# Scan products on quadrants of TensorE, and three steps shifted, in a two-layer perceiver kernel

## The chip, the cores and the metric

The kernel runs on one core of one Trainium2 chip. The metric is the device time of one execution in microseconds (us), taken as the median of several runs. A core has a matrix engine (TensorE, PE in the profile, with PEld for its weight loads), a vector engine (VectorE, DVE), an activation engine (ScalarE, ACT), a general engine (GpSimd, POOL) and a queue engine (SyncE, SP) that here issues most of the transfers. Each engine works through its own instructions in order; semaphores join them. Matrix products go to PSUM, a small memory in banks of 512 f32 per partition, and are read from there by DVE or ACT.

## The reference

Sixteen batches of 64 latent tokens (128 wide, `x`) pass through two layers. Each layer is a cross attention to a context of 1601 tokens, a sequence model (a scan) and a feed-forward part; each part adds to `x`. The first layer has a scan of 16 states per channel and a mixture of experts with a small attention of its own, the second a scan with 4 heads and a feed-forward part with 4-bit quantization. Cut to what matters here:

```python
x = x + L0_xattn(ctx, layernorm(x), ...)     # 16 heads, latents attend to context and latents
x = x + L0_attn(layernorm(x), ...)           # scan of the first layer
x = x + L0_ffn(layernorm(x), ...)            # 4-head attention over 64 tokens, then 8 experts, 2 used
x = x + L1_xattn(ctx, layernorm(x), mask, ...)
x = x + L1_attn(layernorm(x), ...)           # scan of the second layer, below
x = x + L1_ffn(layernorm(x), ...)            # 4-bit quantized gate, up, down

def step(h, inp):                            # L1_attn, one token, per batch and head
    x_t, dt_t, B_t, C_t = inp
    h = exp(A * dt_t) * h + dt_t * B_t * x_t
    y_t = einsum('bhpn,bhn->bhp', h, C_t) + D * x_t
    return h, y_t
```

The scan of the second layer can be written without a loop. For tokens s <= t of the same batch, y_t is the sum over s of (C_t . B_s) times exp(A times the sum of dt over s+1..t) times dt_s x_s. The kernel does it in this form: a matrix of decays, a matrix of products C times B, their product where s <= t in the same batch, and one matrix product with dt x.

## The kernel before

Two batches of 64 tokens make one chunk of 128 tokens; there are eight chunks. All matrix products are in f32, and each shows up as two records of PE and two of PEld.

**The attention is the beat.** `run` counts steps n. One group is a batch and half of its heads; it has 13 steps, one per tile of 128 context rows, and there are 64 groups, 32 per layer. In a step `scores` makes one 128 by 512 product (tile `s`, three PSUM buffers of their own), DVE keeps a running maximum `R` and ACT copies the scores to `st`. A maximum is turned and spread (`tm`, `mb`), `weigh` subtracts and exponentiates, and 21 steps (`LAG`) after the scores `average` weighs the values: four products of 128 by 129 (tile `av`). The big `st` tiles have twelve buffers under the tag `st2`.

**The rest is put between.** Everything else is written as generators. `prep` holds those with a step at which they begin (weights folded, context loaded and normalized, queries). `between` holds the first layer's `scan0` and `moe`, for four groups of two chunks each, and then the second layer's `scan1` and `ffn`, for chunks 0-1, 2-3, 4-5, 6 and 7. Those in `between` run strictly one after the other. A step adds a budget, at most 2.0 of it is kept; a generator that yields a number takes that much of it, and one that yields a tuple (`HOP1` is `(1,)`, `HOP3` is `(3,)`) is not called again before so many steps have passed. `prep`'s generators are called once per step, and a tuple makes them skip steps. The `behind` context places what a generator issues behind the matmuls of the attention already issued, so its place in each engine's order follows from the step in which it is called. Loads go to SP and have no such tie to the attention. After the last step the remaining generators are run out as a tail: the last chunk's `scan1` and `ffn` run alone there, with filler matmuls (`fill`) between.

**PSUM for all but attention's scores and averages** is `tp`: one tag, three buffers of one bank each. Scans, experts, transposes and folds share it. A fourth request waits until an earlier tile is read.

**Lines that the change touches.** Lines 274 to 287 (`setup_rest`) build two 128 by 128 masks on POOL: `upto` (1 where s <= t in the same batch) and `after` (1 where s > t in the same batch). Lines 323 to 352 (`fold`) load a pair of raw weights with `raw_pair` and multiply them per head; `fold_vo(0)` begins at step 9, makes W_v times W_o for the first layer in four turns, and waits `HOP3` between a turn's loads and its products. Each pair sits in one of the twelve `st2` buffers. The first reader of the folded product is the first attention output, at step 81. In `moe`, lines 974 to 986 make queries (`mq`), keys (`mk`) and values (`mv`) of its small attention one after the other, each in a `tp` tile that ACT copies out. `scan1` does this for a chunk c:

- line 1272: `af` = `after` times A dt, a head per 128 columns (DVE)
- lines 1295 to 1301: `gr` = B times C with heads of the same half i of the partitions in one `tp` tile; DVE multiplies by `upto` into `gm`
- lines 1304 to 1310: `seg` = `af` times `upto`, the sums of A dt; ACT exponentiates into `af`
- line 1320: `gm` = `gm` times `af` (DVE)
- lines 1326 and 1329: `sy` = `gm` times `xd` (dt x), added to `y`

In the last chunk the exponential and line 1320 are done in two halves (`parts`), two heads each. Since a chunk holds two batches, half of each 128 by 128 block of `af` and `gm` is zero.

## Time and profile before

| | us |
|---|---|
| median of 3 runs | 1975.37 (1974.5 to 1977.61) |
| the profiled execution | 1973.36 |
| its span, first to last instruction | 1971.6 |
| steps 0 to 416, layer 1's scores begun | 11.5 to 952.2 |
| last score | 1902.9 |
| `moe`, first group | 475.2 to 577.7 |
| `moe`, last group | 1352.5 to 1452.4 |
| `scan1`, chunks 0-1, 2-3, 4-5 begin | 1459.8, 1567.9, 1741.2 |
| last `scan1` | about 1936 to 1954.5 |

The profile is of one execution. Its page gives the busy time of each engine and the costliest groups of instructions by line; the trace behind it can be asked for the busy time in a stretch, for the instructions in order of time (start, length, engine, line, operation, output and inputs, shape, and in brackets how long the engine stood idle before and for whom), and for the chain of work that ended last. A matmul line merges the records of one source line; `x8` is four f32 matmuls. Matmuls are pipelined, so the length of a merged line reaches beyond the start of what follows; what a block of matmuls costs PE is read from start to start.

### The profile page before, as it was taken

The numbers are of one execution on the slowest core, as the hardware profiler recorded it, in microseconds if no ns is written. First come the engines' busy times: TensorE is split into PE (matmuls) and PEld (weight loads), VectorE is DVE, ScalarE is ACT, GpSimd is POOL, SyncE is SP. The second block draws the span as 40 slices with busy tenths as digits, with TensorE's granted clock in tenths as the row PEclk, the third lists the DMA queues.
The fourth block names the chain that finished last, engine by engine and source line by source line (L and its number), as shares of the span: only waits on it lengthen the run. The fifth ranks groups of instructions, "written<-read, shape, count | busy, mean of one in ns | idle before, by whom it ended". The sixth has DMA issues, their size and how long they took to land. (4 is left out here: it accounts for less than half of the span.)

```text
span 1971.6 us, 32642 instructions
## 1 busy us (share of the span) xinstructions
PE 1931.2 (98%) x11987; PEld 1478.8 (75%) x11987; DVE 1582.9 (80%) x3029; ACT 1383.5 (70%) x2638; POOL 512.3 (26%) x579
## 2 busy tenths in 40 slices
PE   8999999999999999999999999999999999999998
PEld 5777777677777767777777777777778777787786
DVE  6977776987878887876998878898786978778875
ACT  5888787887868878666776657776665665766651
POOL 5211122543123452121452202542110111101000
PEclk9999999999999999999999999999999999999999
DMA  6121112322122221221221112221120210201000
GB/s 184 46 68 51 39 54 77 85 67 70 35 76 85 66 77 53 67 78 59 77 82 54 41 40 64 70 58 54 49 67 1 58 37 19 59 18 37 23 1 23
DMA packets 146223, 111.86 MB, mean 57 GB/s; under 512 B 13827, under 2 KB 132367, under 8 KB 146063
## 3 DMA queue, kind: packets, MB, share of 16 engines
q1 hardware_dynamic: 145518, 109.51, 19.1%
q8 instruction: 95, 1.56, 0.3%
q14 instruction: 66, 0.53, 0.1%
q10 hardware_dynamic: 544, 0.26, 0.0%
HBM read 81.28 MB, written 27.41 MB: 55 GB/s over the span
## 5 line engine op out<-in xcount | busy, mean ns | idle before, releaser
L760 PEld LDWEIGHTS av<-kv,st 128*128 128x128 f32 x6656 | 870.0, 192 | 376.6 <-issue 357.5
L760 PE MATMUL av<-kv,st 128*128 128x129 f32 x6656 | 881.8, 275 | 4.0 <-DVE aq L769 4.0
L697 PE MATMUL s<-qT,kvT 128*128 128x512 f32 x1664 | 859.3, 599 | 7.4 <-ACT st L712 5.5
L748 ACT ACTIVATE st<-st 128x1024 f32<-128x1024 f32 (+1 forms) x448 | 444.3, 996 | 120.7 <-DVE st L747 114.1
L747 DVE TENSOR_TENSOR st<-st,mb 128x1024 f32<-128x1024 f32 (+1 forms) x448 | 503.7, 1134 | 17.9 <-PE mb L739 17.9
L710 ACT ACTIVATE st<-s,mcol 128x512 f32<-128x512 f32 x416 | 283.2, 684 | 191.3 <-DVE R L705 167.6
L712 ACT COPY st<-s 128x512 f32<-128x512 f32 x416 | 240.0, 580 | 133.6 <-DVE R L707 121.4
L705 DVE SCALAR_TENSOR_TENSOR R<-s,mcol,R 128x512 f32<-128x512 f32 x352 | 262.2, 745 | 43.9 <-PE s L697 42.4
L707 DVE TENSOR_TENSOR R<-s,R 128x512 f32<-128x512 f32 x352 | 241.0, 685 | 61.9 <-PE s L697 59.8
L697 PEld LDWEIGHTS s<-qT,kvT 128*128 128x128 f32 x1664 | 254.5, 192 | 21.6 <-ACT st L712 10.3
L613 POOL TENSOR_TENSOR kv<-kv,vec 128x384 f32<-128x384 f32 (+1 forms) x128 | 131.8, 1050 | 149.5 <-PE kt L672 36.2
L809 POOL TENSOR_TENSOR aq<-aq,rd 128x512 f32<-128x512 f32 x63 | 74.4, 1181 | 341.4 <-DVE rd L808 329.9
L913 POOL TENSOR_TENSOR db<-sc_u,bb 128x512 f32<-128x512 f32 x64 | 83.7, 1310 | 120.2 <-DVE h L924 63.4
L930 POOL TENSOR_TENSOR sc_y<-sc_y,h 128x512 f32<-128x512 f32 x60 | 81.9, 1365 | 116.6 <-DVE h L929 100.0
L924 DVE TENSOR_TENSOR_SCAN h<-da,db 128x512 f32<-128x512 f32 x64 | 91.8, 1434 | 0.5 <-ACT da L912 0.5
L663 ACT ACTIVATE kv<-kv,coff,crstd 128x128 f32<-128x128 f32 x182 | 76.2, 490 | 6.0 <-POOL coff L660 6.0
L769 DVE SCALAR_TENSOR_TENSOR aq<-xeb,ee,av 128x129 f32<-128x129 f32 x252 | 76.3, 341 | 0.0
L654 ACT ACTIVATE scr<-kv,cmean 128x128 f32<-128x128 f32 x182 | 72.7, 399 | 2.8 <-DVE cmean L650 0.6
L135 POOL TENSOR_TENSOR crstd<-cvar,neghalf 128x13 f32<-128x13 f32 x14 | 34.2, 2440 | 138.1 <-DVE cvar L658 137.7
L490 PE MATMUL q<-xnT,wqk 128*128 128x128 f32 x512 | 68.1, 276 | 0.8 <-ACT qT L499 0.8
L490 PEld LDWEIGHTS q<-xnT,wqk 128*128 128x128 f32 x512 | 62.7, 192 | 4.1 <-issue 1.6
L681 ACT ACTIVATE kvT<-kvT,vcol 128x768 f32<-128x768 f32 (+1 forms) x62 | 58.2, 959 | 3.9 <-DMA xhT<-kvT 3.9
(419 smaller groups left out, 1896.7 us busy)
## 6 DMA issues: line engine op xcount, KB each, us to landing
bb<-bcd SPq DMA_DIRECT2D x64, 256.0 KB, 4.4
xh<-kv SPq DMA_DIRECT2D x16, 832.0 KB, 4.7
kv<-xh SPq DMA_DIRECT2D x16, 832.0 KB, 5.6
kvT<-xhT SPq DMA_DIRECT2D x16, 800.0 KB, 4.6
xhT<-kvT SPq DMA_DIRECT2D x15, 800.0 KB, 3.4
kv<-in_ctx_dram SPq DMA_DIRECT2D x15, 768.0 KB, 5.6
ew<-in_e1T_dram SPq DMA_DIRECT2D x36, 64.0 KB, 1.9
ew<-in_e3T_dram SPq DMA_DIRECT2D x36, 64.0 KB, 2.0
```

What stands on the lines that cost most here:

```text
L490: nc.tensor.matmul(t[:, k * P:(k + 1) * P], self.wqk[:, g * 4 + k, :], xnT, start=True, stop=True)
L613: nc.gpsimd.tensor_tensor(kv[:, lo:hi, :D], kv[:, lo:hi, :D], self.row(self.vec[:, w1, :], [P, hi - lo, D]), ALU.mult)
L697: mm = nc.tensor.matmul(s, self.kv_of[lay, b][1][:, i * P:(i + 1) * P], q, start=True, stop=True)
L705: mx = nc.vector.scalar_tensor_tensor(R, s, mc, last, ALU.add, ALU.max)
L707: mx = nc.vector.tensor_tensor(R, s, last, ALU.max)
L710: ev = nc.scalar.activation(st, s, AF.Identity, bias=mc)
L712: ev = nc.scalar.copy(st, s)
L747: nc.vector.tensor_tensor(st, st, self.row(mb, [P, n, NQ]), ALU.subtract)
L748: nc.scalar.activation(st, st, AF.Exp)
L760: nc.tensor.matmul(grp["av", j][:, k, :], st, self.kv_of[lay, b][0][:, i, :], start=(i == 0 and k == 0), stop=(i == NT - 1 and k == 1))
L913: nc.gpsimd.tensor_tensor(db, u, self.row(bb[:, 0, s % 2, :], both), ALU.mult)
L924: nc.vector.tensor_tensor_scan(flat(h), flat(da), flat(db), 0.0, ALU.mult, ALU.add)
```

## The change

In `scan1` the zero half of the blocks is no longer made. Masks, `af` and `gm` keep 64 columns per head: row p holds token p of its chunk, and the columns are the 64 tokens of p's own batch. The products `gr`, `seg` and `sy` are issued per batch b: the operands of batch b lie on partitions 64 b to 64 b + 63, and the output goes to the same partitions. So each of them becomes twice as many products with 64 columns of weights (`gr`: i chooses the input partitions and b the output partitions; `seg` and `sy`: b chooses both). `gr` takes both of its `tp` tiles before its first product. The last chunk's halves (`parts`) are gone. The numbers yielded are smaller (0.7 to 0.4 per chunk for `af`, 0.9 to 0.6 for `gr`, 0.8 to 0.5 for line 1320), and a `HOP1` stands between the first and the second chunk's `gr`.

In `moe` a yield of 0.3 and a `HOP1` stand between keys and values. In `fold` the first layer's W_v waits five steps instead of three between loads and products. `setup_rest` makes the two masks in 128 by 64 form, with two selects of 64 by 64 each.

```diff
-        self.upto = self.cst([P, P], "upto")
-        nc.gpsimd.memset(self.upto, 1.0)
-        nc.gpsimd.affine_select(
-            out=self.upto, in_=self.upto, compare_op=ALU.is_ge, fill=0.0, base=0,
-            pattern=[[1, P]], channel_multiplier=-1,
-        )
-        nc.gpsimd.memset(self.upto[0:64, 64:128], 0.0)
...
+        self.upto, self.after = self.cst([P, L], "upto"), self.cst([P, L], "after")
+        for t, op, sign in ((self.upto, ALU.is_ge, 1), (self.after, ALU.is_gt, -1)):
+            nc.gpsimd.memset(t, 1.0)
+            for b in range(2):
+                half = t[b * L:(b + 1) * L]
+                nc.gpsimd.affine_select(
+                    out=half, in_=half, compare_op=op, fill=0.0, base=0,
+                    pattern=[[sign, L]], channel_multiplier=-sign,
+                )
...
             if lay == 0 and l == "WvT":
-                yield HOP3
+                yield (5,)
...
             nc.scalar.copy(kT, t[:, :TG])
+            yield 0.3
+            yield HOP1
             t = self.tp("mv")
...
-            parts = ((0, 2), (2, NH)) if last else ((0, NH),)
-
-            full = [P, NH, P]
+            full = [P, NH, L]
+            both = [slice(b * L, (b + 1) * L) for b in range(2)]
...
-            yield 0.6 + 0.7 * CG
+            yield 0.6 + 0.4 * CG
...
-                tok = slice(c * P, (c + 1) * P)
+                gs = [self.tp(f"gr{c}{i}") for i in range(2)]
+                for k in range(2):
+                    for i in range(2):
+                        part = slice(i * HD, (i + 1) * HD)
+                        for b in range(2):
+                            tok = slice(c * P + b * L, c * P + (b + 1) * L)
+                            nc.tensor.matmul(gs[i][both[b], k * L:(k + 1) * L], bT[part, k, tok], cT[part, k, tok], start=True, stop=True)
                 for i in range(2):
-                    g = self.tp(f"gr{c}{i}")
-                    part = slice(i * HD, (i + 1) * HD)
-                    for k in range(2):
-                        nc.tensor.matmul(g[:, k * P:(k + 1) * P], bT[part, k, tok], cT[part, k, tok], start=True, stop=True)
                     gi = gm[c].rearrange("p (k i) t -> p i k t", i=2)[:, i]
-                    nc.vector.tensor_tensor(gi, g[:, :2 * P].rearrange("p (k t) -> p k t", k=2), self.row(self.upto, [P, 2, P]), ALU.mult)
-                yield 0.9
+                    nc.vector.tensor_tensor(gi, gs[i][:, :2 * L].rearrange("p (k t) -> p k t", k=2), self.row(self.upto, [P, 2, L]), ALU.mult)
+                yield 0.6
+                if c + 1 < CG:
+                    yield HOP1
             for c in range(CG):
-                for lo, hi in parts:
-                    sg = self.tp(f"seg{c}")
-                    for h in range(lo, hi):
-                        mm = nc.tensor.matmul(sg[:, h * P:(h + 1) * P], af[c][:, h, :], self.upto, start=True, stop=True)
-                    if last and hi == NH:
-                        self.fill(2, mm)
-                    decay = nc.scalar.activation(af[c][:, lo:hi, :].rearrange("p h t -> p (h t)"), sg[:, lo * P:hi * P], AF.Exp)
+                sg = self.tp(f"seg{c}")
+                for h in range(NH):
+                    for b in both:
+                        mm = nc.tensor.matmul(sg[b, h * L:(h + 1) * L], af[c][b, h, :], self.upto[b], start=True, stop=True)
+                if last:
+                    self.fill(2, mm)
+                decay = nc.scalar.activation(af[c].rearrange("p h t -> p (h t)"), sg[:, :NH * L], AF.Exp)
                 yield 0.1
...
-                for lo, hi in parts:
-                    nc.vector.tensor_tensor(gm[c][:, lo:hi, :], gm[c][:, lo:hi, :], af[c][:, lo:hi, :], ALU.mult)
-                yield 0.8
+                nc.vector.tensor_tensor(gm[c], gm[c], af[c], ALU.mult)
+                yield 0.5
...
                 for h in range(NH):
-                    mm = nc.tensor.matmul(o[:, h * HD:(h + 1) * HD], gm[c][:, h, :], xd[:, c, h, :], start=True, stop=True)
+                    for b in both:
+                        mm = nc.tensor.matmul(o[b, h * HD:(h + 1) * HD], gm[c][b, h, :], xd[b, c, h, :], start=True, stop=True)
```

More of the change, by code (lines that the diff above doesn't have):

```diff
@@ L272, in setup_rest @@
         nc.vector.tensor_scalar_mul(self.na1, self.na1, -1.0)
-        self.upto = self.cst([P, P], "upto")
-        nc.gpsimd.memset(self.upto, 1.0)
-        nc.gpsimd.affine_select(
-            out=self.upto, in_=self.upto, compare_op=ALU.is_ge, fill=0.0, base=0,
-            pattern=[[1, P]], channel_multiplier=-1,
-        )
-        nc.gpsimd.memset(self.upto[0:64, 64:128], 0.0)
-        self.after = self.cst([P, P], "after")
-        nc.gpsimd.memset(self.after, 1.0)
-        nc.gpsimd.affine_select(
-            out=self.after, in_=self.after, compare_op=ALU.is_gt, fill=0.0, base=0,
-            pattern=[[-1, P]], channel_multiplier=1,
-        )
-        nc.gpsimd.memset(self.after[64:128, 0:64], 0.0)
+        self.upto, self.after = self.cst([P, L], "upto"), self.cst([P, L], "after")
[7 more added lines that the diff above has]
+                )
         iota_i = self.cst([P, NE], "iota_i", I32)
```

## The prediction

> **What bounds the kernel.** I read the page's busy shares first, then busy times by stretch, then the timeline of TensorE (PE) around each edited line.

> ```profile
> PE 1931.2 (98%) x11987; PEld 1478.8 (75%) x11987; DVE 1582.9 (80%) x3029; ACT 1383.5 (70%) x2638; POOL 512.3 (26%) x579
> ...
> 1640.00:1760.00 120.00, 119.11 (x738) 91.49 (x737) 92.90 (x159) 78.70 (x122) 13.99 (x17) 1.00 0.14 39
> 1760.00:1905.00 145.00, 145.00 (x911) 112.12 (x911) 122.23 (x244) 91.03 (x142) 16.27 (x25) 1.00 0.07 21
> 1905.00:1972.00 67.00, 58.65 (x411) 51.48 (x409) 38.16 (x110) 17.99 (x38) 4.99 (x9) 1.00 0.06 17
> ```

> Columns of the stretches: length, then busy PE, weight loads, DVE, ACT, POOL. A matmul record lasts 275 ns though the next starts 112 ns later, so I checked PE by starts: with 112 ns for 128 columns and 431 ns for 512, the matmuls fill 97.6% of 1530 to 1905 us. In layer 2, where `scan1` runs, PE is the bound until 1905 us, at granted clock 1.00; a microsecond off PE is a microsecond off the time. From 1933 us the last `scan1` and `ffn` are a serial tail.

> **The scan's matmuls.** Chunk 6 stands free of stalls:

> ```profile
> 1890.73 1.05 PE L760 MATMUL av<-kv,st 128*128 128x129 f32 x8
> 1891.71 0.72 PE L1299 MATMUL gr<-sd_cT,sd_bT 64*128 64x128 f32 x8
> 1892.37 1.13 PE L697 MATMUL s<-qT,kvT 128*128 128x512 f32 x2
> 1893.33 0.61 PE L760 MATMUL av<-kv,st 128*128 128x129 f32 x4
> 1893.77 1.06 PE L1307 MATMUL seg<-upto,af 128*128 128x128 f32 x8
> 1894.67 0.61 PE L760 MATMUL av<-kv,st 128*128 128x129 f32 x4
> ...
> 1898.17 1.00 PE L1326 MATMUL sy<-sd_xd,gm 128*128 128x64 f32 x8
> 1899.01 1.08 PE L697 MATMUL s<-qT,kvT 128*128 128x512 f32 x2
> ```

> An f32 matmul is two records. `seg` holds PE from 1893.77 to 1894.67, 0.90 us; `sy` about as long (8 x 112 ns), although it streams only 64 columns: its 128-column weight load sets the pace. `gr` costs 1892.37 - (1890.73 + 8 x 0.112) = 0.74 us: two row halves in parallel, four waves of 112 ns, and 0.30 us around them. Sum 2.54 us a chunk.

> The new 64x64 products have no row; the nearest is `moe`'s 32x64 product with 64 columns:

> ```profile
> 1083.86 1.05 PE L760 MATMUL av<-kv,st 128*128 128x129 f32 x8
> 1084.85 0.69 PE L998 MATMUL ms<-mo_kT,mo_q 32*64 32x64 f32 x32
> 1085.47 1.12 PE L697 MATMUL s<-qT,kvT 128*128 128x512 f32 x2
> ```

> 32 records go through in 0.72 us (1085.47 less 1083.86 + 0.90): four row groups start 6 to 7 ns apart, a wave every 58 ns, so 8 waves = 0.46 us and 0.25 us around them. [...] The trace agrees: entering `ms` or `gr`, a start comes 205 ns after `av` instead of 112; leaving costs about 90 more. `seg` and `sy` pay it newly.

> After the change `seg` and `sy` have 16 records each on two diagonal quadrants: 8 waves. `gr` has 16 records on all four. That two quadrants of one row group overlap is in no row here; if they do, 4 waves, if not, 8. [...]

> Per pair of chunks I count four blocks (`gr` first; `gr` second with the first `seg`; `seg`; both `sy`): 4 x 0.25 + 40 waves x 0.058 = 3.33 us against 5.08 now, 1.75 less. Chunk 6: 3 x 0.25 + 20 x 0.058 = 1.92 against 2.54, 0.62 less. Three pairs and chunk 6: **5.8 us** (4.2 with 8 waves in `gr`). DVE drops from 512 to 256 elements in `af` and `gm` (0.69 to about 0.42 us, as the tail's half products of 256 elements), from 256 to 128 in `gr`'s eviction; some 0.8 us a chunk, worth nothing by itself while PE is the bound.

> **The step between chunks.**

> ```profile
> 1604.10 2.02 DVE L1272 TENSOR_TENSOR af<-after,sd_adt 128x512 f32<-128x512 f32 x2
> ...
> 1606.51 0.77 PE L1299 MATMUL gr<-sd_cT,sd_bT 64*128 64x128 f32 x4 [1.84 <-DVE gm L1301]
> ```

> The second chunk's `gr` finds no free PSUM slot of three, since `gm`'s eviction is queued on DVE behind both `af`. By block lengths the pairs lose 0.5, 2.5 and 0 us: 3.0. With a step (about 2.3 us) between, and `af` halved, that wait should be over. Next late is the second `seg`, which needs a slot that `gm` of that chunk frees; only the first `seg` (0.6 us) and two evictions of about 0.28 us lie between, and PE's scores are queued behind it. If DVE is then in one of its 1.2 us subtractions, up to 1.2 us a pair returns. I take **2.3** (0 to 3.0).

> **Keys and values apart.**

> ```profile
> 1082.23 0.63 PE L984 MATMUL mv<-w_fWkvT,mo_xT 128*128 128x32 f32 x4 [1.27 <-ACT mo_q L977]
> ```

> `mv` waits for the slot that ACT's copy of `mq` frees: 1.43 us beyond the normal start here, 0.9 near 483 us, none in the other two groups. A step later ACT has done its copies: **1.9** (0 to 2.3). Everything of `moe` behind it, its DMA requests on SP and its POOL additions included, moves by a step. Expert weights have three buffers and were already requested near 481 us, before `mv` ran. The four groups follow each other without a break, so from 484 us the scan and MoE work stands one to four steps later against the attention; `scan1`'s third pair has slack: it may not start before step 759 and the stage ahead of it ends near 731.

> **Raw W_v.**

> ```profile
> 36.28 0.49 ACT L641 ACTIVATE kv<-kv,coff,crstd 128x128 f32<-128x128 f32 x1 [2.51 <-POOL coff L636]
> ...
> 36.77 1.14 PE L344 MATMUL WvT<-rawWvT 64*128 64x128 f32 x8 [1.82 <-DMA rawWvT<-in_L0Wo_dram]
> ```

> A second wait at 48.37 us is 0.65: 2.5 in all. The first product moves two steps back, while its transfer leaves SP as before. But what then comes first is late too: ACT is blocked until 36.28 us, so only one of three score buffers is free, and PE meets that wait after one score. About half remains: **1.2** (0 to 2.5). A turn takes six steps instead of four; the last product falls at step 32 instead of 24 and the first reader at 81, so that is covered. Each turn holds one of the twelve `st2` buffers longer, against scores that just fit: that is the 0 end.

> **Masks** are built by as much POOL time (1.3 us near 25 us): nothing.

> **The tail.**

> ```profile
> 1945.77 0.69 DVE af L1272
> 1946.46 0.34 DVE sd_z L1274
> 1946.85 1.16 PE seg L1307 x8
> 1948.01 0.87 PE fill L130 x4
> 1948.88 0.85 PE sy L1326 x8
> 1949.82 0.43 DVE sd_y L1329
> ```

> `af` gives 0.27. Then eight waves and the result (0.7), one exponential instead of two halves (0.38), one product (0.43), `sy` (0.75) and five hand-overs of 0.04 to 0.06: about 2.5 from `seg` to `sd_y` where 2.97 stand. **0.8** (0.3 to 1.0).

> **Sum.** 5.8 + 2.3 + 1.9 + 1.2 + 0.8 = 12.0 us. The profiled execution took 1973.36 us around a span of 1971.6; that gives 1961.4. The median shown is 2.0 above it, so 1963.4; I say **1963.5**.

> **Rivals.**
> *Quadrants in turn.* If the quadrants don't overlap, each block is 16 x 0.058 + 0.25 = 1.18 us; per chunk 3.54 against 2.54, less 0.25 saved in each pair twice: +5.5 us over seven chunks. With the other edits' 5.4 us and an unchanged tail: 1975.5. Against it stand `gr`'s row halves and `ms`'s row groups, which overlap. 10%.
> *Realignment makes it slower.* Moved by one to four steps from 484 us on, the scan and MoE work asks for the three PSUM slots in other steps than now, and meets context transposes and query products there. Between 60 and 1450 us such stalls cost PE 49 us. A collision is worth 1.1 to 1.5 us, as at `mv`; it decides once they cost over 16 us more than now, some 13 more. With 18 more: 1981.5. For it: 136 starts of the scores are now over 60 ns late, by such alignments; against it: a shift should remove as many as it makes. 10%.
> *Small edits hidden.* PE gains, but other waits take over those of `gr`, `mv` and W_v: 5.8 + 0.8 gives 1968.8. 17%.
> Forecast: 63%.

> **Numbers.** The forecast's own range, from its terms' ends (gains of 14.6 and 4.5), is 1961 to 1971. Realignment by up to 6 us either way widens it to **1955 to 1976**, which takes in the second and fourth case. A measurement of this kernel tells 0.2%, 4 us, from no change. Forecast and hidden edits are mostly faster: 0.77; same 0.13, mostly quadrants in turn; slower 0.10.

> **What would show it.** `seg` and `sy` with 16 records in about 0.7 us; `gr` with 16 in about 0.5 (0.7: one row group's quadrants take turns); no wait of `gr` on `gm` nor of `mv` on `mo_q`; `WvT` without a DMA wait, and the scores behind it waiting instead; `seg` to `sd_y` in the tail 2.5 us. Blocks over 1.1 us, or new waits of the scores from 484 us on, would make the prediction wrong.

## The result, and the profile after

The median is 1967.32 us (8 runs, 1965.93 to 1969.17), against 1974.48 (8 runs) for the kernel before: a ratio of 0.9969 [0.9960, 0.9978], 7.2 us less. The profiled execution took 1967.71 us around a span of 1966.0; before it was 1973.36 around 1971.6, so the trace has 5.6 us to account for. The forecast was a gain of 12.0 us and a time of 1963.5 us.

The first line of the page, and a stretch of layer 2 (length, then busy PE, weight loads, DVE, ACT, POOL, granted clock, DMA):

```profile
PE 1923.6 (98%) x12179; PEld 1470.5 (75%) x12179; DVE 1572.4 (80%) x3028; ACT 1381.5 (70%) x2637; POOL 513.3 (26%) x579
```

```profile
1760.00:1905.00 145.00, 144.85 (x1010) 112.07 (x1009) 120.41 (x244) 90.27 (x139) 16.26 (x25) 1.00 0.08 21
```

PE still hardly rests there and issues 99 records more in these 145 us. The gain in the matmuls is real. The timeline of PE around chunk 6 shows it (start, length, line, shapes, count):

```profile
1886.26 1.05 PE L755 MATMUL av<-kv,st 128*128 128x129 f32 x8
1887.25 0.46 PE L1298 MATMUL gr<-sd_cT,sd_bT 64*64 64x64 f32 x16
1887.64 1.12 PE L692 MATMUL s<-qT,kvT 128*128 128x512 f32 x2
...
1892.47 1.05 PE L755 MATMUL av<-kv,st 128*128 128x129 f32 x8
1893.45 0.68 PE L1328 MATMUL sy<-sd_xd,gm 64*64 64x64 f32 x16
1894.06 1.12 PE L692 MATMUL s<-qT,kvT 128*128 128x512 f32 x2
```

With 8 x 0.112 us for `av`, `gr` costs 1887.64 - 1886.26 - 0.90 = 0.48 us (0.74 before) and `sy` 0.69; `seg`, by the same count, 0.71 (0.90). In the trace the four quadrants' records start 6 to 7 ns apart and the waves, after the first, 58 ns apart, so the two quadrants of one row group do overlap in `gr`.

In the tail, from the chain of waits, `seg` to `sd_y` takes 2.51 us:

```profile
1941.67 0.68 PE seg L1309 x16
...
1943.42 0.67 PE sy L1328 x16
1944.18 0.43 DVE sd_y L1331
```

What the forecast did not have is a loss early in layer 2. POOL, DVE and PE around the first `scan1`'s transposes (in brackets the idle time before, and for whom), first in the kernel before, then after:

```profile
1461.98 0.70 POOL L135 TENSOR_TENSOR rstd<-var,neghalf 128x2 f32<-128x2 f32 x1
1462.72 0.60 DVE L162 TENSOR_SCALAR sd_xi<-X,mv,rstd 128x128 f32<-128x128 f32 x2 [0.47 <-POOL rstd L135]
1464.32 0.38 PE L177 MATMUL sdt<-ident,sd_xi 128*128 128x128 f32 x2
1470.07 3.87 POOL L613 TENSOR_TENSOR kv<-kv,vec 128x512 f32<-128x512 f32 x4 [1.40 <-DMA kv<-xh]
```

```profile
1465.34 1.19 POOL L608 TENSOR_TENSOR kv<-kv,vec 128x512 f32<-128x512 f32 x1 [1.74 <-DMA kv<-xh]
1466.62 0.19 POOL L155 TENSOR_SCALAR var<-mv 128x2 f32<-128x2 f32 x1
1466.89 0.96 POOL L608 TENSOR_TENSOR kv<-kv,vec 128x384 f32<-128x384 f32 x1
1467.80 0.70 POOL L135 TENSOR_TENSOR rstd<-var,neghalf 128x2 f32<-128x2 f32 x1
1468.54 1.83 DVE L162 TENSOR_SCALAR sd_xi<-X,mv,rstd 128x128 f32<-128x128 f32 x2 [2.71 <-POOL rstd L135]
...
1469.65 0.30 PE L177 MATMUL sdt<-ident,sd_xi 128*128 128x128 f32 x1 [2.01 <-DVE sd_xi L162]
```

The layernorm's two small POOL operations (0.19 and 0.70 us) stand in POOL's queue behind multiplications of the context (line 608), the first of which waits for a DMA. DVE waits for them, PE for DVE, and the next scores stand behind PE's transposes. DVE's two `sd_xi` then run beside further multiplications (POOL, from 1468.47 us) and take 1.83 us instead of 0.60. Before, `rstd` came first, and the transposes had no wait. Now they come 2.18 and 0.66 us later than the starts' pitch.

The first `ffn`'s transposes (`fft`) are 3.34 us late. From `qxx` on no POOL operation stands in their chain. DVE works through it, up to `ff_xi` for which PE waits, while POOL multiplies:

```profile
1537.18 4.36 POOL L608 TENSOR_TENSOR kv<-kv,vec 128x512 f32<-128x512 f32 x4 [0.21 <-DMA kv<-xh]
...
1537.51 1.13 DVE L1371 TENSOR_TENSOR qxx<-ff_xi,qxri 128x256 f32<-128x256 f32 x1
1538.56 0.92 DVE L446 TENSOR_SCALAR se<-se,mex 128x8 f32<-128x8 f32 x1
...
1539.80 0.97 DVE L1374 SCALAR_TENSOR_TENSOR qxw<-qxx,qxt 128x256 bf16<-128x256 f32 x1
...
1540.99 0.82 DVE L1376 SCALAR_TENSOR_TENSOR qxt<-qxx,qxw 128x256 f32<-128x256 f32 x1
...
1544.67 0.41 PE L177 MATMUL fft<-ident,ff_xi 128*128 128x128 f32 x2 [3.18 <-DVE ff_xi L1382]
```

In the kernel before these four DVE operations take 0.42, 0.22, 0.42 and 0.42 us, with POOL's multiplications not or hardly beside them. Here they are 2.4 us longer together, most of the wait.

That is not the whole price. Busy times in stretches of 2 us behind the wait of `fft` (the third number from the right is the granted clock), and PE's timeline there:

```profile
1544.00:1546.00 2.00, 1.32 (x5) 0.73 (x6) 2.00 (x4) 2.00 (x4) 0.00 (x0) 0.91 0.84 317
1546.00:1548.00 2.00, 2.00 (x11) 2.00 (x10) 1.59 (x3) 2.00 (x4) 0.00 (x0) 0.50 0.11 37
1548.00:1550.00 2.00, 2.00 (x10) 1.40 (x9) 0.87 (x2) 0.79 (x2) 0.00 (x0) 0.74 0.00 0
```

```profile
1545.93 1.93 PE L755 MATMUL av<-kv,st 128*128 128x129 f32 x8
1547.65 1.06 PE L716 MATMUL tm<-ident,R 128*128 128x128 f32 x4
```

Eight records of `av` take 1547.65 - 1545.93 = 1.72 us instead of 0.90. The clock is 0.50 for 3.4 us, which costs 1.7 us, once after `sdt` and once after `fft`. The kernel before has two such stretches too, at other places: after `WvT`'s wait at 36.77 us and after `gr`'s at 1606.51, where its first `seg` took 1609.07 - 1607.20 = 1.87 us:

```profile
1607.20 2.08 PE L1307 MATMUL seg<-upto,af 128*128 128x128 f32 x8
1609.07 1.72 PE L760 MATMUL av<-kv,st 128*128 128x129 f32 x8
```

The page's clock row cannot show them: its slices are 49 us long and read 9 throughout.

PE's time from step 572 to the last score, split by the starts of its matmuls; a record is late when its start comes over 0.25 us later than the pitch of the one before allows:

| us | before | after | `no_moe_step` | `quads_only` | `in_turn` | `six_later` |
|---|---|---|---|---|---|---|
| all other matmuls at their pitch | 574.4 | 574.4 | 574.3 | 574.4 | 574.2 | 574.4 |
| `gr`, `seg`, `sy`, entering included | 19.7 | 11.6 | 12.0 | 12.7 | 14.4 | 11.8 |
| late starts | 7.9 | 10.5 | 5.9 | 7.3 | 9.8 | 1.8 |
| the rest: small delays, half clock | 5.0 | 6.9 | 4.5 | 5.2 | 7.1 | 5.1 |
| sum | 606.9 | 603.4 | 596.6 | 599.6 | 605.5 | 593.0 |

The scan's matmuls gave 8.1 us (about 1 of it the slow `seg` of before), and 4.5 of that went back into late starts and half clock. Ahead of step 572 the kernel after is 1.4 us better, and behind the last score 0.75.

### The profile page after: what moved, and what is told of

Its sections match the earlier page's. It is cut to its first block, busy times and chain, and to the rows that moved or that the text cites. A ratio compares the mean times of both kernels' runs of the same rounds, so it can differ in the third digit from the quotient of the medians.

```text
span 1966.0 us, 33029 instructions
## 1 busy us (share of the span) xinstructions
PE 1923.6 (98%) x12179; PEld 1470.5 (75%) x12179; DVE 1572.4 (80%) x3028; ACT 1381.5 (70%) x2637; POOL 513.3 (26%) x579
## 5 line engine op out<-in xcount | busy, mean ns | idle before, releaser
L692 PEld LDWEIGHTS s<-qT,kvT 128*128 128x128 f32 x1664 | 255.2, 192 | 24.5 <-ACT st L707 14.2
L702 DVE TENSOR_TENSOR R<-s,st 128x512 f32<-128x512 f32 x32 | 22.0, 686 | 57.5 <-PE s L692 55.1
```

Of the source, the lines that this page charges most:

```text
L692: mm = nc.tensor.matmul(s, self.kv_of[lay, b][1][:, i * P:(i + 1) * P], q, start=True, stop=True)
L702: mx = nc.vector.tensor_tensor(R, s, last, ALU.max)
```

## The experiments

Each ratio is to the kernel before, run on the same chip. "Last score" is the start of step 831 in the trace against the one of before, so it leaves the tail out.

| run | median, us | ratio [95%] | last score, us |
|---|---|---|---|
| after | 1967.32 | 0.9969 [0.9960, 0.9978] | -4.9 |
| `after_again` | 1966.91 | 0.9961 [0.9948, 0.9973] | -5.7 |
| `quads_only` | 1967.08 | 0.9970 [0.9958, 0.9981] | -5.6 |
| `only_moe_step` | 1975.24 | 1.0011 [1.0004, 1.0017] | +2.3 |
| `no_moe_step` | 1963.72 | 0.9950 [0.9937, 0.9962] | -11.2 |
| `no_chunk_step` | 1966.66 | 0.9964 [0.9952, 0.9977] | -6.0 |
| `wv3` | 1967.38 | 0.9970 [0.9959, 0.9981] | -3.5 |
| `in_turn` | 1970.70 | 0.9989 [0.9982, 0.9995] | -2.6 |
| `one_tile` | 1962.61 | 0.9945 [0.9931, 0.9958] | -11.9 |
| `six_later` | 1959.32 | 0.9930 [0.9918, 0.9943] | -14.2 |
| `one_tile_ten` | 1960.65 | 0.9930 [0.9917, 0.9944] | -11.5 |
| `busy_wait` | 1965.71 | 0.9963 [0.9950, 0.9976] | -6.2 |
| `busy_half` | 1965.31 | 0.9961 [0.9947, 0.9975] | -8.2 |

**The step between keys and values.** `no_moe_step` is the kernel after without it:

```diff
             nc.scalar.copy(kT, t[:, :TG])
-            yield 0.3
-            yield HOP1
             t = self.tp("mv")
```

> The changed kernel without the yield of 0.3 and the one-step wait between keys and values in moe. Theory (alignment): the four added steps pushed the first scan of layer 2 and its ffn onto POOL's context multiplications; that cost PE 2.84 us at the scan's first transposes and 3.34 at the ffn's, so both waits go, 6.2 us, and the values' wait on the queries' copy comes back with 1.4 to 2.3: about 1962.5 to 1963.5 beside a changed kernel of 1967.3. Rival (the values' step is worth its price, the two waits are of the scan's own making): both waits stay and the values' wait is added, 1968.7 to 1969.6.

`only_moe_step` is the kernel before with these two yields added and nothing else.

> The kernel before with that step between keys and values alone. Alignment: a wait of the values on the queries' copy (1.43 us near 1082) goes, but the first scan of layer 2 starts some four steps later as in the changed kernel and meets the same POOL work: its transposes wait about 2.8 us; net slower by 1 to 4 us, 1975.5 to 1978.5 beside 1974.5. Rival: faster by 1.4 to 2.3, 1972.2 to 1973.1.

Without the step the kernel after is faster, and its interval lies almost wholly below the one of after (it overlaps that of `after_again`); with nothing but the step the kernel before is slower, by 0.11%, 2.2 us. In `only_moe_step` the waits of `sdt` appear in the kernel before (2.15 us late at 1470.16), and a start of the scores comes 3.87 us late at 1547.84; in `no_moe_step` neither exists, `rstd` runs at 1460.84 us and the context's multiplications at 1468.88. So the step makes the collision. What it was to save is small: from step 221, ahead of the first group, to step 572, in the last, `only_moe_step` gains 0.2 us. One execution does not settle so little: over the same steps the kernel after gains 0.2 us and `after_again`, the same kernel, 1.1. On average the eight traces with the step gain 0.3 us on the kernel before and the four without it (the one before among them) lose 0.3, so the step is worth about 0.6 us, within a spread of 1.8. The wait of 0.9 us near 483 us went to context transposes (`kt`, 0.89 late), and for the one of 1.43 at 1082 us came `mot` (0.68) and `xnt` (1.64, at 1105.89).

**Keys and values in one tile**, which takes that wait away with no step:

```diff
-            nc.scalar.copy(kT, t[:, :TG])
-            yield 0.3
-            yield HOP1
-            t = self.tp("mv")
...
-                nc.tensor.matmul(t[:, c * 32:(c + 1) * 32], xT[:, c * P:(c + 1) * P], fWkvT[:, 32:], start=True, stop=True)
+                nc.tensor.matmul(t[:, TG + c * 32:TG + (c + 1) * 32], xT[:, c * P:(c + 1) * P], fWkvT[:, 32:], start=True, stop=True)
+            nc.scalar.copy(kT, t[:, :TG])
...
```

> The changed kernel without the step in moe, with the values' product written to free columns of the keys' PSUM tile, so that it asks for no fourth buffer and needs no step. Theory (the values waited for a buffer): the waits near 483 and 1082 us (0.9 and 1.43 us) go, and no stage moves by a step: 1.4 to 2.3 us faster than without the step in moe, 0.9939 to 0.9943 of the kernel before. Rival (some other product meets the same full buffers instead): 0.995.

The wait near 1082 us is gone and nothing comes for it; of the one near 483 us, 0.62 us remains, at `kt`. It gains 0.7 us between the same two steps, again less than executions differ. Its interval overlaps that of `no_moe_step`, so the times do not tell the two apart.

**The meeting on POOL.** `six_later` keeps the whole change and starts the first `scan1` six steps later:

```diff
             if CG == 1 and not last:
                 self.shifted_weights(inT)
+            if c0 == 0:
+                yield (6,)
             yield from self.layernorm(xi, X, CG, last)
```

> The changed kernel, step in moe included, with the first scan of layer 2 held back by six steps before its layernorm. Theory (alignment with POOL's context multiplications): the 2.84 us wait of the scan's first transposes goes, since POOL is past that context; the ffn's wait of 3.34 us goes too or another takes its place: 2.8 to 6.2 us faster than the changed kernel, 0.9938 to 0.9955 of the kernel before. Rival (the waits belong to the scan wherever it stands): they stay, 0.997.

Its timeline of POOL:

```profile
1466.33 3.87 POOL L608 TENSOR_TENSOR kv<-kv,vec 128x512 f32<-128x512 f32 x4 [1.67 <-DMA kv<-xh]
...
1473.59 0.70 POOL L135 TENSOR_TENSOR rstd<-var,neghalf 128x2 f32<-128x2 f32 x1
```

Now `rstd` is behind the multiplications. The two `sd_xi` take 0.60 us and `qxx` 0.42 again, `sdt` and `fft` come without a wait, and the clock is 1.00 from the start to the tail. From step 572 to the last score it is 10.3 us faster than the kernel after, more than the 6.2 expected, since the half clock goes with the waits. By the median this is the fastest kernel of the case. By the table it keeps what the step in `moe` does well (`me`, 1.82 us late at 1414.52 before, and a late `mb` of 1.67 at 1305.91 are gone or halved) without the collision: from step 572 one start is over half a microsecond late, by 0.86. `one_tile_ten` puts a delay of ten steps on `one_tile`:

> The run with the values in the keys' tile, with the first scan of layer 2 held back by ten steps, so that it stands at the same steps as in the run held back by six (which has four more in moe). Alignment: layer 2 as in that run (0.993 of the kernel before), and layer 1 without its waits for the values' buffer, up to 1.5 us less: 0.9922 to 0.993. Rival (that run's gain came from layer 1's own shift): 0.9945, as with the values in the keys' tile alone.

It has no collision at the scan either, but `me` comes 2.02 us late at 1412.06, with 3.4 us of half clock behind it. So the two together bring nothing beyond the delay alone.

**The half clock.** `busy_wait` puts matmuls of the identity ahead of the two late transposes, into the tile that the transposes then overwrite; `busy_half` uses 4 and 7 of them:

```diff
         t = self.tp(name)
+        for _ in range({'sdt0': 8, 'fft0': 14}.get(name, 0)): nc.tensor.matmul(t[:, :P], self.ident, self.ident, start=True, stop=True)
         for k in range(n):
```

> The kernel after, with 8 matmuls of the identity (0.224 us each, 1.8 us) issued ahead of the first scan's transposes and 14 (3.1 us) ahead of the first ffn's, into the tile that the transposes then overwrite. TensorE is busy while it waits there; the waits for DVE are as long as they were. Theory that the waits' price is doubled by the clock: the granted clock is 0.5 for 3.4 us after each of the two waits in the kernel after, and stays 1.00 here; each stretch gives back 1.7 us, so the span is 3.4 below the kernel after (about 1962.5) and the ratio to before about 0.995. Rival, that the half clock comes from something else at those places (the context's loads, DVE, the steps of the work): the clock falls as in the kernel after, and the time is 0.9965 of before. Third, that the fillers are longer than the waits and only displace work: slower than the kernel after by up to 1 us with the clock at 1.00 and no gain.

> The same with 4 and 7 of these matmuls (0.9 and 1.6 us), so that TensorE still stands idle for about 1.3 and 1.8 us. Of all kernels so far single waits of up to 1.9 us outside the start were followed by full clock and those of 2.0 and more by 3.4 us at half clock. If it is the idle time that counts, against a border of about 2 us, the clock stays at 1.00 as with all waits filled, and the time is the same, 3.4 us below the kernel after. If it is the wait as a whole or the place, the clock falls as in the kernel after and nothing is gained. In between, one of the two stretches: 1.7 us.

PE's timeline of `busy_half`:

```profile
1543.25 0.44 PE L177 MATMUL fft<-ident,ff_xi 128*128 128x128 f32 x2 [1.63 <-DVE ff_xi L1382]
...
1544.38 1.05 PE L755 MATMUL av<-kv,st 128*128 128x129 f32 x8
1545.28 0.60 PE L716 MATMUL tm<-ident,R 128*128 128x128 f32 x4
```

The transposes come as late as ever, but `av` takes 0.90 us, and the clock stays at 1.00 in both kernels. From step 640 to step 690, over both waits, `busy_wait` needs 3.4 us less than the kernel after and `busy_half` 3.2, of which 1.6 come behind each wait: the 3.4 expected. So at these two places it is PE's idle time that brings the half clock, and it costs as much as expected. The ratios did not reach the 0.995 of the expectation and overlap with after's. A reason lies in the other executions: the mean clock of the kernel after's runs, here and in `after_again`, goes from 0.997 (1969.17 us) to 1.000 (1963.82), so not every one has both stretches. `busy_wait` also lost 2.4 us against the kernel after ahead of step 572 in its profiled execution. The runs of the two lie within 1.9 us, those of the kernel after within 5.4.

**The scan's matmuls.** `quads_only` is the kernel before with the quadrants alone: the old numbers yielded, no step between chunks or in `moe`, `HOP3` for W_v.

> The kernel before with the products on quadrants alone: old yields, no step between chunks, none in moe, W_v asked for three steps ahead. By my count of blocks (5.8 us of TensorE in the body, 0.8 in the tail) 6.6 us faster than before: 0.9967. If the quadrants also end the pairs' waits, up to 3 more: 0.9950. If the quadrants' gain is hidden behind the vector engine, less than 3 us: over 0.9985.

It gains 7.3 us from step 572 to the last score, nearly all in the scan's row of the table. `in_turn` is the kernel after with the two loops of `seg` and `sy` exchanged:

```diff
-                for h in range(NH):
-                    for b in both:
+                for b in both:
+                    for h in range(NH):
```

> The changed kernel with the batch as the outer loop in the decay sums and in the product with dt x: all eight records of one quadrant first, then all eight of the other. If records start in program order, a quadrant's records follow each other and nothing overlaps: a block takes 16 x 0.058 + 0.25 = 1.18 us instead of 0.72, 0.46 more for each of 14 blocks in the body, 6.4 us slower, and some 0.9 in the tail: 1974.6 beside 1967.3. If each quadrant has a queue of its own, no change: 1967.3.

Its timeline of PE:

```profile
1894.45 1.05 PE L755 MATMUL av<-kv,st 128*128 128x129 f32 x8
1895.43 0.96 PE L1328 MATMUL sy<-sd_xd,gm 64*64 64x64 f32 x16
1896.33 1.12 PE L692 MATMUL s<-qT,kvT 128*128 128x512 f32 x2
```

The same 16 records now take 1896.33 - 1894.45 - 0.90 = 0.98 us instead of 0.69. Less 0.25 us around them, that is about 13 waves of 58 ns instead of 8: by this count the two quadrants overlap in three records only. The full overlap, 0.69 us, came with neighbours in the queue on different quadrants. The expectation, with no overlap, had 1.18 us and 6.4 us in the body; neither it nor its rival, no change, came. In the scan's row it costs 2.8 us, by the two ratios 0.2%, 3.9 us, and their intervals do not meet.

**The step between the chunks.** `no_chunk_step` is `no_moe_step` without `if c + 1 < CG: yield HOP1` as well.

> The changed kernel without the step in moe and without the step between two chunks' C times B. My prediction gave that step 2.3 us (0 to 3.0). If it is what removes the wait of C times B on its own evictions, that wait returns at one or more of the three pairs, 1 to 3 us slower than the run without the step in moe (0.995 of the kernel before): 0.9955 to 0.9965. Rival: the shorter columns and the halved decay tables have already emptied the vector engine's queue, and the step is worth nothing: 0.995.

`gr` is 0.59 us late in it and 0.70 in `no_moe_step`, which has the step; in `quads_only`, with the old numbers yielded, 1.60. It is the smaller work and the smaller yields that took most of that wait away. `no_chunk_step` has another wait instead (`syt` on `sd_y`, 2.03 us late at 1783.15, with half clock behind). The intervals of the two overlap, so what the step is worth stays open.

**W_v.** `wv3` is the kernel after with `HOP3` in place of the five steps.

> The changed kernel with three steps instead of five between the loads of raw W_v and their products. The steps of the scores in the two traces differ by 1.15 us from step 52 to step 221, so I expect 1.2 us back: 1968.5 beside 1967.3. Rival: the shift has effects further on (the buffers of the scores, the order on SP), then 2 us or more either way.

The times do not tell it from after. The traces do: at step 52 the four kernels with three steps (the one before among them) stand on average 0.3 us behind the kernel before (0.6 ahead to 0.9 behind), the ten with five 0.8 ahead of it (0.2 to 1.5). All four with three have one stretch of half clock ahead of 65 us (at 36 or 58 us), none of those with five has one there.

**The kernel after again:**

> The changed kernel itself, on the same chip as the run beside it: 0.9969 of the kernel before, as measured; its trace shows the waits of 2.8 and 3.3 us at the first scan's transposes and the ffn's again, if they are set by the order of the program and not by the execution.

The waits of `sdt` and `fft` come back at the same steps: 2.16 and 0.66, and 3.35 us late.

## Why the prediction was right, and where it was wrong

The time fell inside the range, and much of the mechanism of the forecast was right: PE is the bound, and what comes off it comes off the time. The sum was 12.0, and the trace holds 5.6. It is the 6 us allowed for realignment that kept the time inside a range of 21 us; by the number alone the rival "small edits hidden" (6.6 us) was nearer than the forecast, by chance, since more than that was gained and part of it lost again. Of the signs named, `seg`, `sy`, `gr`, `mv` and the tail came as said; `WvT` without a DMA wait did not, and the new waits that were to speak against the prediction came, at the transposes in front of the scores.

- **Scan's matmuls, 5.8:** right. Pairs of chunks cost 3.20, 3.20 and 3.31 us (forecast 3.33), chunk 6 1.89 (1.92). Block by block that is 17.8 less 11.6, 6.2; the forecast's own terms, 3 x 1.75 + 0.62, give 5.9. The remainder is that in two pairs the second `seg` follows the first directly, without a product of the attention between, where the forecast had two blocks. Going from `gr` to `seg`, both on quadrants, costs nothing, as the forecast had it: the next start comes 38 or 39 ns later. Around the blocks the trace shows what the rows of before showed for `ms` and `gr`: a start 205 ns after `av` instead of 112 on entering, about 90 more on leaving, nothing from `gr` to `seg`. Four waves for `gr` was an estimate of the author that no row of the kernel before shows; after, the block takes 0.48 us, which is 0.25 + 4 x 0.058. That the quadrants overlap was the choice on which the rival "quadrants in turn" hung; it depends on the order of issue (`sy` 0.69 us, 0.98 in `in_turn`).
- **Step between chunks, 2.3:** the waits went (3.0), and 1.7 of half clock behind them, which the forecast did not count. That the step did it is not shown; by `no_chunk_step` and `quads_only` it was mostly the smaller work and yields.
- **Keys and values apart, 1.9:** wrong; 0.2 in this trace, about 0.6 by the means above. The step removes the wait but other waits take its place: the rival "small edits hidden", right for this edit alone.
- **W_v, 1.2:** 1.1, by the step-52 means. The size was right, but not the way: the wait for the DMA was to go, and of its 1.82 us 1.21 remain. Only the second wait is gone. The half clock behind the first, 1.7, is avoided, which was not named, and waits of the scores give part of it back:

```profile
36.18 0.71 PE L339 MATMUL WvT<-rawWvT 64*128 64x128 f32 x8 [1.21 <-DMA rawWvT<-in_L0Wo_dram]
37.23 1.12 PE L692 MATMUL s<-qT,kvT 128*128 128x512 f32 x2 [0.34 <-ACT st L707]
```

- **Masks 0, tail 0.8:** right; the tail 0.75 (the forecast's own terms add up to 0.74).
- **Realignment, valued at nothing, 6 either way:** this is the step that failed. "A shift should remove as many as it makes" holds for the number of waits. From step 572 on the shift took away `me` (1.82), half of `mb` (0.80), a wait of the scores (0.57) and `ft` (1.05), 4.2 us, and made `sdt` (2.84), `fft` (3.34) and `tm` (1.39), 7.6. But two of the new ones left PE idle for over 2 us, and each is followed by 3.4 us at half clock, 3.4 us more. That is 6.7 net. The rival for realignment put the collision at the three PSUM slots and at 1.1 to 1.5 us each. It was at POOL's context multiplications, and twice as dear: `sdt` waits for short operations in POOL's queue and then for DVE's two `sd_xi`, 1.83 us beside POOL instead of 0.60, `fft` for four DVE operations that take 2.4 us more beside POOL. Its point of decision, 16 us, was not reached.

Together: 6.2 + 3.0 + 1.7 + 0.2 + 1.1 + 0.75 - 6.7 = 6.3, against 5.6 in the trace.

The forecast had no half clock. In the traces its depth is 0.50 and its length 3.413 us, and in each trace the changes of the clock lie whole multiples of 3.413 us apart (after: 1470.53 and 1545.62, 22 of them; before: 36.90 and 1607.03, 460), at other places in each execution: counted from the first instruction, 2.8 us past such a multiple in before and after, 1.1 in `wv3`, 0.1 in `only_moe_step`.

How much idle time goes ahead of it can be read too. I divided each trace into windows of 3.413 us on this grid, up to the last score, and added up PE's idle time by its starts in each window at full clock. Windows with up to 2.00 us were followed by full clock, all but two; those with 2.12 us or more by half clock, all of them; between lie three (2.07, 2.10, 2.11) that were followed by half clock and one (2.11) that was not. So in these traces about 2.1 us of 3.413 were enough. The idle time within one window tells the cases apart, the length of a wait does not. Single waits of 2.00 us (`gr`, before), 2.02 (`me`, `one_tile_ten`) and 2.03 (`syt`), each inside one window (2.11 to 2.21 in it with the small delays beside), brought half clock. A score of `six_later` comes 2.02 us late at 741.06 us, its wait is split between two windows, the larger sum is 1.84, and the clock stays at 1.00. A score of `busy_half` comes even 2.26 us late, a window ends 0.63 us into its wait, the next one's sum is the 2.11 named last, and the clock stays at 1.00 too:

```profile
740.07 1.12 PE L692 MATMUL s<-qT,kvT 128*128 128x512 f32 x2 [2.10 <-ACT st L707]
```

```profile
740.00:742.00 2.00, 1.57 (x6) 0.90 (x6) 0.77 (x2) 2.00 (x4) 0.20 (x1) 1.00 0.00 0
742.00:744.00 2.00, 1.55 (x8) 1.08 (x9) 1.96 (x4) 2.00 (x4) 0.13 (x1) 1.00 0.29 83
```

That fits executions of one kernel that differ in their stretches of half clock. The two exceptions are the stretches from 59 us on in `quads_only` and `wv3`: the window ahead holds no wait of PE, but 14 matmuls of only 16 columns (`mskT`). Why half clock follows them stays open.

## What to carry to other kernels

Where work is interleaved by a fixed count of steps, a step added anywhere moves everything behind it; before adding one, follow each engine's queue at the new place, and look for short operations of a chain that fall behind long ones that wait for a transfer, and for DVE chains that run beside long POOL operations (four operations took 2.4 us more here). Where TensorE was the bound in these traces and idled for more than about 2.1 us within one window of 3.413 us, 1.7 us of half clock came on top. So cutting such a wait below 2 us, or filling part of it with matmuls that do nothing (1.6 us back behind each of the two in `busy_half`), was worth more than its own length. A wait of 2.00 us (`gr`, before) brought it and one of 2.26 us (a score, `busy_half`) did not, by where the window ended. When products are split over quadrants, issue neighbours on different quadrants (`sy` took 0.69 us so and 0.98 otherwise), and put blocks of the same form side by side (38 or 39 ns from `gr` to `seg`, 205 from `av` to either).
